# A graph-network layer on one core: the convolution's columns cut 128 + 6 x (133 or 134) instead of 116 + 6 x (135 or 136)

## The chip, the cores and the metric

The kernel runs on one core of a Trainium2 chip. The metric is the device time of one execution in microseconds, as the median of several runs. Engines are named as the profile names them: PE (TensorE matmuls), PEld (its weight loads), DVE (VectorE), ACT (ScalarE), POOL (GpSimd) and SP (SyncE, which issues most of the DMAs).

## What is computed

The input `x` has 32 batches of 512 nodes with 256 features, and `adj` is a 512 x 512 mask for each batch. All is in float32. Cut to what matters:

```python
h  = relu(layernorm(x))
# conv branch, along the nodes
c  = relu(bn1(conv1(h)))             # 1 tap, 256 -> 256
xc = relu(bn2(conv2(c)) + h)         # 17 taps, padding 8
# graph branch
s  = h @ w_se.T + b_se               # 3 numbers per node
A  = exp(-dist(s, s)) * adj
xn = A @ relu(h @ w_msg.T + b_msg)
# gates
gi = concat(xc, xn) @ w_ih.T + b_ih ; gh = h @ w_hh.T + b_hh
r, z = sigmoid(gi_r + gh_r), sigmoid(gi_z + gh_z)
out = x + (1 - z) * tanh(gi_n + r * gh_n) + z * h
```

## The kernel before

**The convolution by columns.** The 17-tap convolution is done with 25 products per group of columns in place of 17 (a bilinear scheme with five points, twice, on top of a split into two phases). A unit is 18 consecutive nodes (`Q = 18`), a batch has 29 units (`U = 29`), and the 32 batches give 928 columns in one row. `STARTS` cuts these 928 columns into seven groups, and cuts need not fall between batches; a batch on a cut has columns in two groups. `batches(g)` lists the batches that group `g` touches.

For each group, in this order:

- `rows(g, b)` calls `conv1(g, b, o)` for each batch and output half: PE multiplies `w1` by the batch's normalized, transposed rows (`hT`, [128 x 2 x 512]) into a `ps_g` bank, and ACT writes the result with batch norm and relu into `h1`, the one buffer that holds the group's input. In group 0 the rows are still in SBUF; in the others `load_row` loads them again from the DRAM copy `hd` (512 KB, on SP's queue). The tile `hT` has two buffers, also used when a batch is first transposed.
- `operands(g)` makes the 25 operands (`x2`, and for groups above 0 also their difference `xd`) on DVE from `h1`. It can begin when all rows of the group are there (`made`), and the next group's rows can be written when the last outer operand of this one has been read (`freed`). At most three operands are made ahead (`AHEAD = 3`).
- `convolution()` runs the 25 products into `ps_c`. Group 0 takes two half products of 8 matmuls each per operand (4 each for the operand `LONE`), while the weights are still being made on DVE and ACT; the later groups take three products of 4 matmuls (two for `LONE`) with weights that SP loads back from DRAM (`w<-wd`). Each matmul has as many columns as the group.
- `summed(g)` adds the products up on ACT and DVE (`n`, `z`, `y`), and `evacuate()` writes them as `part` and, on POOL's queue, to DRAM as `cd`.

**The other work.** `begin(b)` normalizes batch `b` and turns it into `hT` and `hd`: by PE transposes for the first eight batches (`TURNED = 8`; the tiles `x_sb`, `x_odd` and, for batches 2 and 3, `y`), by DVE for the rest. `graph(b)` makes messages (`wmsg`), the kernel's exponentials (`right`, `left`), multiplies by the mask (`m_sb`, tile `at`) and gathers (`at,msg`). `gates(b)` does the gates (`ps_acc`), in a form with fewer products (`wsum`, `t`) for all batches but the first and last. It begins when the weights of group 0 are made.

**What sets the order.** The program is written out once, by a planner inside the kernel. It keeps an estimated time (`now`) and five streams: rows, begins, graphs, conv and gates. At each step it takes the stream that is furthest behind its due rate among those that could run. Wherever several could run, it counts one (`choices`), and the table `OTHERS` names the counts at which the second or third is taken instead. All engines, and the queues of SP and POOL, then work through that order. When no stream can run, `now` moves on in steps of 0.25 us; before the first gates, every fourth such step issues a 128 x 128 transpose of the identity, which does nothing but keep PE busy (`keep_warm`, line 272, `ps_acc<-ident`).

The streams' use of group 0 is in two places, `all_rows` and `all_begins`: the first `G = 4` batches are begun by the rows stream itself, each followed at once by its rows; all others by the begins stream.

Of the kernel before, what the change touches and what calls it, by code (L numbers as in the profile page):

```python
# [31 lines left out]
G = 4  # L32
U = 29
Q = 18

STARTS = (0, 116, 252, 388, 523, 658, 793, 928)
NG = len(STARTS) - 1
UG = max(j - i for i, j in zip(STARTS, STARTS[1:]))
PER = (STARTS[-1] - STARTS[1]) / (NG - 1) / U
TURNED = 8  # L40
# [10 lines left out]
def kernel(  # L51
# [32 lines left out]
    B, N, D = x.shape  # L84
# [4 lines left out]
    def sizes(g):  # L89


        nu = STARTS[g + 1] - STARTS[g]
        return nu, ND * nu, 2 * ND * nu, ND * (nu + 1)
# [190 lines left out]
    def later(t, f):  # L284
        LATER.append((t, f))
        LATER.sort(key=lambda e: e[0])
# [48 lines left out]
    def load_row(b):  # L335
        if b not in HR:
            settle_stores()
            HR[b] = front.tile([P, ND, N], F32, name="hT", bufs=2)
            sp.dma_start(HR[b], HD[b])
            HR_AT[b] = done(HR[b])  # L340
# [87 lines left out]
    def input_of(g):  # L428
        return h1[:, : Q * sizes(g)[3]].rearrange("p (q i v) -> p q i v", q=Q, i=ND)

    def zeros(g):
        at = input_of(g)
        for b in range(B + 1):
            v = U * b - STARTS[g]
            if 0 <= v <= sizes(g)[0]:
                pool.memset(at[:, : Q if v == sizes(g)[0] else LEAD, :, v : v + 1], 0.0)
                if v > 0:
                    pool.memset(at[:, Q - 1 : Q, :, v - 1 : v], 0.0)
# [91 lines left out]
    def conv1(g, b, o):  # L530

        hT = HT[b] if g == 0 else HR[b]
        v0, at = U * b - STARTS[g], input_of(g)
        first, last = max(0, -v0), min(U, sizes(g)[0] - v0)
# [363 lines left out]
    def batches(g):  # L898

        return range(STARTS[g] // U, (STARTS[g + 1] - 1) // U + 1)  # L900
# [332 lines left out]
    def begin(b):  # L1233

        nonlocal begun, turning
        if b >= TURNED:
            yield lambda: b not in NORMS
            yield NORM_AT[b]  # L1240
            xs = XS.pop(b)
            pool.dma_start(XD_[b].rearrange("(c p) d -> p c d", p=P), xs)
            yield done(XD_[b])
            xb = xs.rearrange("p c d -> p (c d)").rearrange("p (o n) -> p o n", o=ND)
            for o in range(ND):
                blocks(xb[:, o, :], XD_[b].rearrange("(k i) d -> i k d", i=32), o)
            yield max(done(xb), front.free("hT", 2))
            settle_stores()
            HT[b] = front.tile([P, ND, N], F32, name="hT", bufs=2)
            turning = True  # L1250
            for o in range(ND):
                dve.transpose(HT[b][:, o, :], xb[:, o, :])
                if o < ND - 1:
                    yield dve.free
            yield dve.free + 0.4
            pool.dma_start(HD[b], HT[b])
            begun, turning = b + 1, False
            if b + 1 < B:
                later(now + 0.3, lambda: load(b + 1))
            return  # L1260
        if b == 2:
            yield lambda: told > 0
        yield lambda: b not in NORMS
        yield NORM_AT[b]
        turning = True
        for d in range(ND):
            yield gps.free("ps_g")
            norm_t(b, d)
            if d == ND - 1:
                begun, turning = b + 1, False  # L1270
                if b < 2 or G <= b < TURNED - 1:
                    load(b + (G if b < 2 else 2))
            yield now

    def rows(g, b):
        nonlocal made, made_at
        for o in range(ND):
            yield gps.free("ps_g")
            conv1(g, b, o)
            if o == ND - 1 and b == batches(g)[-1]:  # L1280
                made, made_at = g + 1, act.free + LAG
            yield now
        HT.pop(b, None)
# [457 lines left out]
            yield from graph(b)  # L1741

    def all_begins():
        for b in range(G, B):
            yield lambda: b in XS and not rows_wait
            yield from begin(b)

# [1 line left out]

    def all_rows():  # L1750
        nonlocal rows_wait
        for b in range(G):
            yield from begin(b)
            yield act.free + LAG
            yield from rows(0, b)
        for g in range(1, NG):
            for b in batches(g):
                yield lambda: (
                    freed >= g - 1 and begun > b and not turning and at_product >= 25 * g - 4
                )  # L1760
                if b == batches(g)[0]:
                    zeros(g)
                rows_wait = True
                yield front.free("hT", 2) - 0.5
                load_row(b)
                if b + 1 in batches(g) and b + 1 < begun:
                    later(max(now + 2.5, front.free("hT", 2) - 0.5), lambda b=b: load_row(b + 1))
                yield HR_AT[b]
                yield from rows(g, b)
                del HR[b]  # L1770
                rows_wait = b + 1 in HR

    def all_gates():
# [6 lines left out]

    streams = {
        "rows": (all_rows(), 1e9, -2.0),
        "begins": (all_begins(), 1.05 * PER, -0.15),
        "graphs": (all_graphs(), 11.5 * PER, -0.5),
        "conv": (convolution(), 80.0, 0.0),
# [5 lines left out]


    OTHERS = {
        6: 1, 41: 1, 259: 1, 374: 1, 430: 1, 443: 1, 547: 1, 953: 1, 979: 1, 1020: 2,
        1022: 1, 1182: 1, 1202: 1, 1260: 1, 1291: 1, 1471: 1, 1636: 1, 1670: 1, 1744: 1,
        1745: 1, 1837: 1, 2031: 1, 2149: 1, 2232: 1, 2391: 1, 2604: 1, 2610: 1,
    }
    choices = 0
    unused, waits = acc.tile([P, N], F32, name="ps_acc"), 0
# [113 lines left out]
```

## Time and profile before

| | |
|---|---|
| median of 3 runs | 2008.96 us (2005.38 to 2012.02) |
| the profiled execution | 2015.27 us, of which its span is 2013.5 us |
| PE busy, DVE busy, ACT busy, POOL busy | 1973.8, 1505.0, 874.1, 478.5 us |
| mean granted clock of PE | 0.991 of full speed |
| group 0's products | from 55.5 us to 232.8 us |
| windows 0:60, 60:234, 234:1815, 1815:2013.5: PE busy | 52.94, 167.75, 1564.16, 188.97 us |
| the same windows: DVE busy | 38.93, 140.07, 1234.71, 91.27 us |

A row of the groups reads: line, engine, operation, output <- input, the tile sizes, the count; then busy time and mean length of one record in ns; then the idle time of the engine just before these, and what ended it. A row of the timeline reads: start, length of the stretch, engine, line, operation, count, and in brackets the idle time before it with what ended it. All matmuls come from the helper line 259 and PE transposes from 265, so groups are told apart by their tiles. A float32 matmul of the code is two records in the trace, each with its own weight load; the start of one to the start of the next is what it costs.

### The profile page before, as it was taken

Reading aid. Unit: us, or ns where it says so; the run is one execution under the profiler, and the core shown is the slowest. Engines: PE = TensorE matmul, PEld = TensorE weight load, DVE = VectorE, ACT = ScalarE, POOL = GpSimd, SP = SyncE. Lnnn points to the kernel's source line nnn. Section 1 sums busy time; section 2 is a strip of 40 time slices with the busy share of each in tenths; the row PEclk is TensorE's granted clock in tenths of the full one; section 3 lists DMA queues with packets and bytes.
Section 4 is the critical chain, followed back from the end, with each engine's and each line's share of the span. In section 5 each row is a group of like instructions: output and inputs, shape, how many; then the busy total and the mean of one; then the engine's idle time right before and its main releaser. Section 6 shows DMA issues by size and latency. Waiting matters only on the chain.

```text
span 2013.5 us, 28526 instructions
## 1 busy us (share of the span) xinstructions
PE 1973.8 (98%) x9692; PEld 1450.8 (72%) x9692; DVE 1505.0 (75%) x2711; ACT 874.1 (43%) x1755; POOL 478.5 (24%) x628
## 2 busy tenths in 40 slices
PE   8999999999999999999999999999999999999998
PEld 5887666776778677776787776777776777776774
DVE  6889589976988597876787775688894877766443
ACT  6644463434634455333464235463334453324321
POOL 3222112222212132222231221232220221113232
PEclk9999899999999999999999999999999999999999
DMA  8446777888898788889787886798895876665564
GB/s 295 168 174 211 238 241 194 211 209 197 227 252 208 194 191 213 200 195 222 146 235 192 204 202 162 191 246 203 179 211 150 185 171 155 157 151 106 111 100 34
DMA packets 578177, 378.92 MB, mean 188 GB/s; under 512 B 457664, under 2 KB 475488, under 8 KB 576896
## 3 DMA queue, kind: packets, MB, share of 16 engines
q1 hardware_dynamic: 419760, 279.15, 49.7%
q0 software_dynamic: 157184, 97.81, 26.4%
q8 instruction: 77, 1.26, 0.2%
q14 instruction: 68, 0.56, 0.1%
q10 hardware_dynamic: 1088, 0.13, 0.0%
HBM read 278.94 MB, written 114.56 MB: 195 GB/s over the span
## 4 chain that ended last, share of the span: by engine, by line
PE 65%; DVE 4%; issue 2%; DMA 1%; ACT 1%; POOL 1%; DVEq 0%; POOLq 0%; SPq 0%; ACTq 0%
PE ps_acc L259 36%; PE ps_c L259 16%; PE ps_g L259 13%; DVE o_sb L241 1%; DMA cd<-part 1%; PE ps_g L265 1%; DVE t L241 0%; POOL out_dram L228 0%; DVE x L241 0%; DMA hd<-hT 0%; POOL cd L228 0%; DVE ps_acc L241 0%; ACT at L241 0%; DVE z L241 0%; DMA w<-wd 0%
## 5 line engine op out<-in xcount | busy, mean ns | idle before, releaser
L228 POOL DMA_DIRECT2D out_dram<-o_sb x252 | 275.8, 1719 | 636.5 <-DVE o_sb L241 510.9
L259 PEld LDWEIGHTS ps_c<-xd,w 128*128 128x128 f32 x2304 | 285.5, 190 | 49.9 <-ACT ps_c L241 33.9
L259 PEld LDWEIGHTS ps_c<-x,w 128*128 128x128 f32 x2032 | 259.8, 194 | 48.2 <-issue 32.9
L259 PE MATMUL ps_c<-xd,w 128*128 128x135 f32 (+1 forms) x2304 | 290.4, 279 | 3.9 <-ACT ps_c L241 3.9
L259 PE MATMUL ps_c<-x,w 128*128 128x135 f32 (+2 forms) x2032 | 268.5, 281 | 2.8 <-DVE x L241 2.8
L259 PE MATMUL ps_g<-at,msg 128*128 128x512 f32 x512 | 230.0, 600 | 3.5 <-DVE at L241 3.5
L241 DVE TENSOR_TENSOR ps_acc<-ps_acc,r 128x256 f32<-128x256 f32 x120 | 51.7, 431 | 230.4 <-PE ps_acc L259 209.3
L259 PE MATMUL ps_acc<-hTb,whh 128*128 128x512 f32 (+2 forms) x532 | 211.4, 495 | 1.4 <-ACT r L241 1.4
L259 PE MATMUL ps_acc<-xconv,wih 128*128 128x512 f32 (+2 forms) x532 | 211.6, 495 | 0.7 <-DVE ps_acc L241 0.7
L259 PE MATMUL ps_acc<-xnb,wih 128*128 128x512 f32 (+2 forms) x532 | 209.1, 496 | 3.2 <-DVE ps_acc L241 3.2
L259 PEld LDWEIGHTS ps_g<-at,msg 128*128 128x128 f32 x512 | 96.9, 193 | 112.8 <-issue 103.4
L259 PE MATMUL ps_acc<-t,wsum 128*128 128x256 f32 x720 | 175.7, 380 | 1.2 <-DVE wsum L241 1.2
L259 PEld LDWEIGHTS ps_acc<-t,wsum 128*128 128x128 f32 x720 | 135.7, 191 | 35.5 <-issue 17.9
L259 PEld LDWEIGHTS ps_acc<-xconv,wih 128*128 128x128 f32 x532 | 98.0, 190 | 48.3 <-issue 38.6
L259 PE MATMUL ps_g<-hT,w 128*128 128x512 f32 (+8 forms) x296 | 124.5, 571 | 7.4 <-DMA hT<-hd 6.8
L259 PEld LDWEIGHTS ps_acc<-xnb,wih 128*128 128x128 f32 x532 | 96.1, 190 | 44.8 <-issue 31.5
L259 PE MATMUL ps_g<-wmsg,hTg 128*128 128x259 f32 x496 | 124.4, 382 | 0.0
L259 PE MATMUL ps_acc<-t,wih 128*128 128x256 f32 x480 | 123.2, 380 | 0.0
L259 PEld LDWEIGHTS ps_acc<-hTb,whh 128*128 128x128 f32 x532 | 94.7, 190 | 38.5 <-issue 28.3
L241 DVE TENSOR_TENSOR x<-x 128x544 f32<-128x544 f32 (+2 forms) x175 | 120.2, 707 | 0.3
L241 ACT ACTIVATE ps_c<-ps_c 128x270 f32<-128x270 f32 (+1 forms) x144 | 56.3, 391 | 137.9 <-PE ps_c L259 137.7
L241 ACT ACTIVATE h<-ps_g,bn_shift,bn_scale 128x252 f32<-128x252 f32 (+8 forms) x212 | 86.3, 484 | 60.4 <-PE ps_g L259 60.4
(157 smaller groups left out, 3251.3 us busy)
## 6 DMA issues: line engine op xcount, KB each, us to landing
w<-wd SPq DMA_DIRECT2D x414, 256.0 KB, 4.0
m_sb<-in_adj_dram SPq DMA_DIRECT2D x384, 64.0 KB, 3.4
wd<-w POOLq DMA_DIRECT2D x74, 256.0 KB, 3.3
hT<-hd SPq DMA_DIRECT2D x33, 512.0 KB, 4.0
hd<-hT POOLq DMA_DIRECT2D x32, 512.0 KB, 6.1
hTb<-hd SPq DMA_DIRECT2D x32, 512.0 KB, 4.6
xnb<-nd SPq DMA_DIRECT2D x64, 256.0 KB, 3.3
out_dram<-o_sb POOLq DMA_DIRECT2D x252, 64.0 KB, 4.8
```

Of the source, the lines that this page charges most:

```text
L228: self.engine.dma_start(dst, src, **more)
L241: getattr(self.engine, op)(*tiles, **more)
L259: nc.tensor.matmul(ps, lhsT, rhs, **more)
L265: nc.tensor.transpose(ps, a, ident)
```

## The change

The first cut moves from 116 (four whole batches) to 128, which is 12 columns into batch 4. The other six groups have 134, 134, 133, 133, 133 and 133 columns where they had 136, 136, 135, 135, 135 and 135. The first group thus touches five batches, and the two places that assumed `G = 4` batches ask `batches(0)` instead, so that batch 4 is begun by the rows stream. `OTHERS` is another table: 51 entries for 27.

```diff
-STARTS = (0, 116, 252, 388, 523, 658, 793, 928)
+STARTS = (0, 128, 262, 396, 529, 662, 795, 928)
...
     def all_begins():
-        for b in range(G, B):
+        for b in range(batches(0)[-1] + 1, B):
             yield lambda: b in XS and not rows_wait
             yield from begin(b)
...
     def all_rows():
         nonlocal rows_wait
-        for b in range(G):
+        for b in batches(0):
             yield from begin(b)
             yield act.free + LAG
             yield from rows(0, b)
...
     OTHERS = {
-        6: 1, 41: 1, 259: 1, 374: 1, 430: 1, 443: 1, 547: 1, 953: 1, 979: 1, 1020: 2,
...
+        85: 1, 89: 2, 121: 1, 157: 2, 194: 1, 260: 1, 280: 1, 344: 1, 347: 1, 404: 1,
...
     }
```

## The prediction, made before the changed kernel was run

> **What bounds the kernel.** I read the page first, then the windows, the groups by form, PE's waits and PE's timeline. TensorE is busy nearly throughout; nothing else is close.
>
> ```profile
> span 2013.5 us, 28526 instructions
> PE 1973.8 (98%) x9692; PEld 1450.8 (72%) x9692; DVE 1505.0 (75%) x2711; ACT 874.1 (43%) x1755; POOL 478.5 (24%) x628
> PE ps_acc L259 36%; PE ps_c L259 16%; PE ps_g L259 13%; DVE o_sb L241 1%; DMA cd<-part 1%; PE ps_g L265 1%; DVE t L241 0%; POOL out_dram L228 0%; DVE x L241 0%; DMA hd<-hT 0%; POOL cd L228 0%; DVE ps_acc L241 0%; ACT at L241 0%; DVE z L241 0%; DMA w<-wd 0%
> ```
>
> The chain of waits is PE work with few interruptions. So a column taken from PE counts in full, and other engines count only where PE waits for them. In the groups by form the convolution's products (ps_c) are:
>
> ```profile
> L259 PE MATMUL ps_c<-xd,w 128*128 128x135 f32 x1536 | 193.0, 279 | 3.2 <-ACT ps_c L241 3.1
> L259 PE MATMUL ps_c<-x,w 128*128 128x135 f32 x832 | 114.4, 282 | 0.0
> L259 PE MATMUL ps_c<-xd,w 128*128 128x136 f32 x768 | 97.4, 279 | 0.8 <-ACT ps_c L241 0.8
> L259 PE MATMUL ps_c<-x,w 128*128 128x116 f32 x784 | 96.8, 281 | 2.8 <-DVE x L241 2.8
> L259 PE MATMUL ps_c<-x,w 128*128 128x136 f32 x416 | 57.3, 281 | 0.0
> ```
>
> The mean of 280 ns is the length of overlapping records and says nothing of their price; the distance of starts does. (The code's 392 matmuls of 116 columns are 784 records: two for each matmul.)
>
> ```profile
> 91.17 1.94 PE L259 MATMUL ps_c<-x,w 128*128 128x116 f32 x16
> 92.95 0.60 PE L265 MATMUL ps_g<-ident,m_sb 128*128 128x128 f32 x4
> ...
> 553.53 2.02 PE L259 MATMUL ps_c<-xd,w 128*128 128x136 f32 x16
> 555.39 1.04 PE L259 MATMUL ps_g<-wmsg,hTg 128*128 128x259 f32 x4
> ```
>
> Sixteen records of 116 columns take 92.95 - 91.17 = 1.78 us, **111.3 ns** each; of 136 columns 1.86 us, **116.3 ns**. Over the trace the median is 115.0 for 135 columns and 429.4 for 512: a slope of 314.4/377 = 0.834 ns per column and 2.4 fixed. By it 116 columns would take 99.1; they take 111.3. Something else sets 12 ns of it, and up to about 130 columns come free.
>
> [...]
>
> ```profile
> 201.76 5.37 PE L259 MATMUL ps_g<-hT,w 128*128 128x512 f32 x8 [2.94 <-DMA hT<-hd]
> 206.96 0.27 PE L265 MATMUL ps_g<-ident,augl 128*128 128x128 f32 x1
> ...
> 237.15 10.20 PE L259 MATMUL ps_g<-at,msg 128*128 128x512 f32 x16 [2.36 <-DVE at L241]
> 247.19 1.04 PE L259 MATMUL ps_g<-wmsg,hTg 128*128 128x259 f32 x4
> ...
> 455.69 10.14 PE L259 MATMUL ps_g<-hT,w 128*128 128x512 f32 x16 [2.33 <-DMA hT<-hd]
> ```
>
> Eight records took 5.20 instead of 8 x 0.429 = 3.43; sixteen took 10.04 and 9.98 (to 465.67) instead of 6.87. So such a wait costs itself and 1.8 to 3.2 us more. These are the places where the convolution passes from one group to the next: the hT row loads (load_row) and the last adjacency mask.
>
> **The change, part by part.** The order of the changed kernel's instructions gives counts.
>
> 1. *Groups 1 to 6.* All of 1536 + 832 + 768 + 416 = 3552 records lose two columns: 3552 x 2 x 0.834 ns = **-5.9 us**, all on PE. At 133 columns the line gives 113.3, still above 111.3, so none of it is cut off. Bounds: if the floor reached 113.3, nothing changes; at 115, all of it is lost.
>
> 2. *Group 0.* 784 records grow from 116 to 128. The line gives 109.2, under the 111.3 paid now: **0**. Not shown in this stream, so bounded: -2.1 ns each (-1.6 us) if the line holds alone, +1.2 (+0.9 us) by the 112.5 of the few 128-column gate matmuls at the end.
>
> 3. *Rows.* Group ends move; batch 4 is now cut, so there is one piece more: 152 instead of 148 conv1 matmuls, 72 more columns (0.1 us) and an 89-column piece that pays the floor (0.3): **+0.4 us**. Row loads stay 33 (before: 37 pieces less 4 from SBUF; now 38 less 5). Two more evacuations on ACT and two more stores on POOL's queue lie beside PE: 43% and 24% busy.
>
> 4. *DVE.* From 638 ns at 468 elements to 717 at 544: 1.04 ns an element. [...] Group 0's operands and sums grow by 6,288 elements: +6.5 us; the others shrink by 7,872: -8.2. PE sees the first only if DVE is late there. DVE is idle 6.8 us in 60:100 and 6.6 in 100:150, which covers it; in 150:200 it is 96% busy and the two DVE waits of 0.56 and 1.75 us stand there. I take +1 (0 to +4).
>
> 5. *The start.* Operands wait for the whole group, which now includes batch 4. Its eight transposes (8 x 0.109) and four conv1 matmuls of 225 columns (8 x 0.19 = 1.5 us) move ahead of the first product (at 55.53 before), and the 0.5 us ACT evacuation and about 2.4 us of DVE operands follow. The order now puts graph 1's masks and gather (6.9 us) ahead of the first product too, where six short products filled PE between 55.5 and 71. Until the gather the new order has only some 5 us of work for about 10 us of latency. It holds eight more warm-up transposes (38 for 30), six of them at the start: 8 x 0.109 = **+0.9 us**, and a sign that its planner finds nothing for PE there. I take **+3** of idleness (1 to 6); the first products' cold clock (3.50 us for 1.78) may come back after it or vanish under the gather.
>
> 6. *Group changes.* Passing 0 to 1 costs now 2.94 + 1.77 (row load), 2.36 + 3.17 (mask), 1.15 of slow clock at 218.74 and 0.6 of short waits: 12.0 us. Passing 1 to 2 costs 0.58 + 2.33 + 3.11 = 6.0. In the new order 7.0 us of PE work, not 2.6, stand ahead of the second row batch of group 1, and four xd products part the last two masks. I take back the first row wait and some of the mask: -7 at 0 to 1. Passing 1 to 2, a load must now land within 4.3 us (below): half recovered, half lost elsewhere, 0. **-7 us** (-12 to +16).
>
> Sum: -5.9 + 0 + 0.4 + 1 + 3 + 0.9 - 7 = **-7.6 us** against the profiled execution's 2015.27 us (span 2013.5 and 1.8 around it): 2007.7. That execution stands 6.3 us over the median of the runs, 2008.96, so the forecast is 2008.96 - 7.6 = **2001.4 us**.
>
> **Rivals.** *The start eats it.* Part 5 at +6, part 6 at -4 because DVE, fed with group 1's long operations, is late for the mask again: -5.9 + 0.4 + 1 + 6 + 0.9 - 4 = -1.6, so 2007.4. For it: the six warm-ups, and the 1.35 us wait that precedes the first product already. Against it: batch 4's work is only moved.
>
> *Slower: exposed row loads.* hT has two buffers, so a row batch's load waits until the batch two before it is done. In the new order seven loads of groups 2 to 5 have only one batch (3.4 us) and about 0.9 us between release and use: 4.3 us. Before, such a load was just in time:
>
> ```profile
> 951.55 3.75 SPq L228 DMA_DIRECT2D hT<-hd  x2
> ...
> 954.79 1.02 PE L259 MATMUL ps_acc<-xconv,wih 128*128 128x512 f32 x2
> 955.68 6.15 PE L259 MATMUL ps_g<-hT,w 128*128 128x512 f32 x16
> ```
>
> Issued at 951.55, used at 955.68: 4.1 us and no wait. The median landing is 4.0, but transfers of hT range from 2.9 to 11.6. Each that is 2.3 us late costs 2.33 + 3.11 = 5.4. With two of the seven late the sum is about +3; with three it is -7.6 + 16.3 = +8.7: **2017.7**, and slower is decided there. Behind such a load SP holds weight loads, and behind PE's rows wait ACT's evacuation and DVE's next operands. Against it: the case above did not wait.
>
> *The cut does not pay.* If the floor holds 133 columns at 115 ns, part 1 is nothing and the sum is -1.7: 2007.3, like the first rival.
>
> **How the numbers follow.** About 0.3% (6.0 us, from 2002.9 to 2015.0) is what a measurement of this kernel tells from no change. The likeliest case is faster, 0.48: its own range is 1994 to 2003, with part 6 near its good end at 1996. The start or the floor eats the gain: 0.31. Exposed loads: 0.21. Leaving a tenth out on either side gives 1995 to 2018.
>
> **What would show it.** ps_c starts 113 to 114 ns apart at 133 and 134 columns and 109 to 112 at 128; a total of PE waits before the first product up by about 3 us; that first product near 72 us, not 55; the 2.94 us wait for hT gone; waits <-DMA hT<-hd otherwise under 7 us in all. I am wrong if 128 columns take over 113 ns, if those waits pass 15 us, or if DVE waits in group 0 exceed 6 us.

## The result, and the profile after

The changed kernel takes **2012.91 us** (median of 20 runs, 2009.14 to 2018.51); beside it on the same chip the kernel before takes 2008.17 us (20 runs, 2003.01 to 2014.92). The ratio is **1.0026**, 95% interval 1.0015 to 1.0036: slower by about 5 us. The prediction was 2001.4 us, and its sign was wrong.

The page after, its head and its chain of waits:

```profile
span 2010.9 us, 28562 instructions
PE 1966.8 (98%) x9708; PEld 1442.8 (72%) x9708; DVE 1500.9 (75%) x2711; ACT 875.9 (44%) x1761; POOL 477.0 (24%) x629
PE ps_acc L259 37%; PE ps_c L259 15%; PE ps_g L259 13%; DMA cd<-part 1%; DMA hT<-hd 1%; DVE o_sb L241 1%; DVE t L241 1%; PE ps_g L265 0%; ACT at L241 0%; ACT y L241 0%; DMA x_sb<-in_x_dram 0%; SPq L228 0%; DVE ps_acc L241 0%; ACT z L241 0%; POOL out_dram L228 0%
```

PE is still the bound at 98%, and busy for 7.0 us less than before. The trap is in the first line: this profiled span is 2.6 us shorter than the span shown of before. The profiled execution of before (2015.27 us) was slower than all 20 of its runs, the one of the change (2012.66) lies at its median. Two single profiles don't rank kernels that are 5 us apart; the runs do.

The convolution's products in the groups by form of the changed kernel (busy, mean ns of a record | idle time just before them and what ended it):

```profile
L259 PE MATMUL ps_c<-xd,w 128*128 128x133 f32 x1536 | 191.6, 277 | 3.8 <-ACT ps_c L241 3.8
L259 PE MATMUL ps_c<-x,w 128*128 128x133 f32 x832 | 112.1, 277 | 0.0
L259 PE MATMUL ps_c<-xd,w 128*128 128x134 f32 x768 | 96.5, 278 | 1.0 <-ACT ps_c L241 0.9
L259 PE MATMUL ps_c<-x,w 128*128 128x128 f32 x784 | 94.6, 276 | 1.2 <-ACT w L241 0.9 <-DVE x L241 0.3
L259 PE MATMUL ps_c<-x,w 128*128 128x134 f32 x416 | 57.0, 281 | 3.0 <-ACT z L241 1.6 <-DVE w L241 1.3
```

The last two rows show what is new. Group 0's products (128 columns) wait for DVE 0.3 us instead of 2.8, but group 1's `x` products, which never waited, now wait 3.0 us for ACT and DVE. The prices stand in PE's timeline after, as distances of starts:

```profile
199.13 3.73 PE L259 MATMUL ps_c<-x,w 128*128 128x128 f32 x32
202.70 2.22 PE L259 MATMUL ps_g<-hT,w 128*128 128x305 f32 x8
...
529.05 2.00 PE L259 MATMUL ps_c<-xd,w 128*128 128x134 f32 x16
530.89 0.59 PE L259 MATMUL ps_acc<-t,whh 128*128 128x256 f32 x2
...
1293.59 1.07 PE L259 MATMUL ps_c<-x,w 128*128 128x133 f32 x8
1294.50 1.04 PE L259 MATMUL ps_g<-wmsg,hTg 128*128 128x259 f32 x4
```

They are 3.57/32 = 111.6 ns for 128 columns, 1.84/16 = 115.0 for 134 and 0.91/8 = 113.8 for 133. Over all neighbouring product records of the trace at full clock the means are 111.7, 114.6 and 114.0, within 0.7 ns of the prediction's floor and line. Before, they are 111.3 for 116 columns, 116.5 for 136 and 115.0 for 135. In groups 1 to 6 that is 2368 x 0.96 + 1184 x 1.95 ns = 4.6 us of PE's time, for 5.9 predicted: over a quarter of the 133-column records take 117 or 118 ns, the rest 112 to 114.

**The start** is another matter. The windows of before, then of the change (the columns are the length, then busy time and records of PE, PEld, DVE, ACT and POOL, then granted clock, DMA share and GB/s):

```profile
0.00:57.00 57.00, 49.94 (x188) 30.43 (x189) 36.18 (x116) 38.13 (x83) 17.02 (x41) 0.96 0.75 275
57.00:80.00 23.00, 23.00 (x145) 18.92 (x145) 20.81 (x40) 9.78 (x24) 4.91 (x8) 0.96 0.43 149
80.00:250.00 170.00, 161.39 (x1007) 126.05 (x1006) 134.49 (x246) 86.10 (x201) 36.94 (x71) 0.96 0.63 208
```

```profile
0.00:57.00 57.00, 49.17 (x184) 29.20 (x184) 32.60 (x111) 38.12 (x84) 16.95 (x41) 0.96 0.74 275
57.00:80.00 23.00, 18.60 (x60) 11.81 (x61) 14.87 (x29) 6.31 (x14) 2.71 (x4) 0.73 0.41 149
80.00:250.00 170.00, 163.83 (x1114) 134.94 (x1113) 145.93 (x257) 91.81 (x216) 38.06 (x73) 1.00 0.57 188
```

Between 57 and 80 us PE was busy throughout before, with 145 records. After it is busy 18.60 us at a clock of 0.73, with 60. Up to 80 us PE thus has 5.2 us more of idleness, and the lower clock costs about (0.96 - 0.73) x 23 = 5 us. From 80 to 250 us the change does better: 163.83 us busy at full clock against 161.39 at 0.96, which is 2.4 us less idleness and about 7 us less of slow clock. So a loss at the start is followed by a gain, most of it at the passage from group 0 to group 1. PE's timeline shows the loss (brackets: idle time before the stretch, and what ended it). First before, then after:

```profile
55.53 3.67 PE L259 MATMUL ps_c<-x,w 128*128 128x116 f32 x16 [0.49 <-DVE x L241]
...
67.42 3.73 PE L259 MATMUL ps_c<-x,w 128*128 128x116 f32 x32
70.99 7.04 PE L259 MATMUL ps_g<-at,msg 128*128 128x512 f32 x16
```

```profile
54.18 0.69 PE L259 MATMUL ps_acc<-right,left 5*128 5x512 f32 x1 [1.25 <-ACT right L241]
...
57.10 1.97 PE L265 MATMUL ps_g<-ident,x_sb 128*128 128x128 f32 x8 [1.40 <-ACT at L241]
...
65.36 0.27 PE L272 MATMUL ps_acc<-ident 128*128 128x128 f32 x1
69.92 10.14 PE L259 MATMUL ps_g<-at,msg 128*128 128x512 f32 x16 [4.29 <-DVE at L241]
79.90 1.28 PE L259 MATMUL ps_c<-x,w 128*128 128x128 f32 x10
```

Graph 1's gather waits 4.29 us for its last mask, and then runs at a granted clock of 0.69 (0.50 up to 76.03 us): 9.98 us to the next start for 6.87. The first product stands at 79.90, not near 72. DVE's timeline in that stretch says why the mask is late:

```profile
65.49 0.39 DVE L241 BATCH_NORM_STATS2 st<-x_sb 128x6 f32<-128x256 f32 x1
...
66.74 0.68 DVE L241 TENSOR_TENSOR at<-ps_g,at 128x512 f32<-128x512 f32 x1
67.34 1.83 DVE L241 TENSOR_TENSOR x<-h 128x1290 f32<-128x1290 f32 x2
69.09 0.69 DVE L241 TENSOR_TENSOR at<-ps_g,at 128x512 f32<-128x512 f32 x1
```

Between the second and the last of the four mask multiplications (`at<-ps_g,at`) stand the next batch's statistics (64.42 to 66.74) and the first two operand instructions of group 0 (`x<-h`, 1.83 us together). Before, the gather came no earlier (70.99), but six products filled PE until then; now the products wait behind the gather, and PE has nothing to do until DVE is through.

And the gain, PE's timeline after at the passage from group 0 to 1:

```profile
202.70 2.22 PE L259 MATMUL ps_g<-hT,w 128*128 128x305 f32 x8
...
211.84 7.03 PE L259 MATMUL ps_g<-hT,w 128*128 128x512 f32 x16
218.70 1.95 PE L259 MATMUL ps_c<-x,w 128*128 128x128 f32 x16
...
247.64 7.13 PE L259 MATMUL ps_g<-at,msg 128*128 128x512 f32 x16 [1.11 <-DVE at L241]
...
256.05 1.15 PE L259 MATMUL ps_c<-x,w 128*128 128x134 f32 x8 [1.27 <-DVE w L241]
```

No row load is waited for, and the mask wait is 1.11 us with a gather at a granted clock of 1.00, where it was 2.36 with one at 0.69: as predicted. But 8 us later a new wait stands, for a weight that DVE makes (and DVE in turn waited 1.99 us for the load `w<-wd`).

**A ledger.** To add this up, I take PE's time up to a point and subtract the price, at full clock, of every record that PE has done by then: the mean distance of starts of its shape, and 0.53 us for four of the exponentials' records, which start within 0.02 us of one another (in the change from 54.18 us, the next four from 54.72). What is left is idleness and slow clock. The second value is that of a second profile (below).

| lost, us | up to 80 us | 80 to 250 us | 250 us to the end |
|---|---|---|---|
| before | 18.0, 18.5 | 18.5, 16.7 | 45.0, 44.2 |
| the change | 28.1, 29.0 | 9.9, 9.9 | 43.9, 52.9 |
| held116 | 19.5 | 18.6 | 38.7 |
| masks128 | 24.3 | 10.8 | 44.3 |
| masks128_stats | 20.6 | 11.4 | 44.2 |
| order128 | 27.5 | 11.5 | 37.7 |
| order128_held | 25.6 | 9.9 | 37.1 |
| order128_stats | 22.1 | 11.5 | 38.2 |

So the change loses about 10 us more than before by 80 us, gets 7 to 9 back by 250, and is then 1 to 4 us behind. The last column varies by 9 us between two executions of one kernel, and both profiles of before are of executions 5 to 7 us over the median of its runs. An estimate at the medians of the runs: PE's work is 1932.0 us before and 1929.1 after, so 74.4 and 82.0 us are lost in all (with 1.8 us around the span), and some 38 and 44 of them behind 250 us. There the change loses about 5 us more.

### The profile page after: what moved, and what is told of

Same layout as the page of the kernel before. It is cut to its first block, busy times and chain, and to the rows that moved or that the text cites. A ratio compares the mean times of both kernels' runs of the same rounds, so it can differ in the third digit from the quotient of the medians.

```text
span 2010.9 us, 28562 instructions
## 1 busy us (share of the span) xinstructions
PE 1966.8 (98%) x9708; PEld 1442.8 (72%) x9708; DVE 1500.9 (75%) x2711; ACT 875.9 (44%) x1761; POOL 477.0 (24%) x629
## 4 chain that ended last, share of the span: by engine, by line
PE 66%; DVE 3%; DMA 2%; issue 2%; ACT 2%; POOL 1%; SPq 0%; DVEq 0%; POOLq 0%; ACTq 0%
PE ps_acc L259 37%; PE ps_c L259 15%; PE ps_g L259 13%; DMA cd<-part 1%; DMA hT<-hd 1%; DVE o_sb L241 1%; DVE t L241 1%; PE ps_g L265 0%; ACT at L241 0%; ACT y L241 0%; DMA x_sb<-in_x_dram 0%; SPq L228 0%; DVE ps_acc L241 0%; ACT z L241 0%; POOL out_dram L228 0%
## 5 line engine op out<-in xcount | busy, mean ns | idle before, releaser
L259 PEld LDWEIGHTS ps_c<-x,w 128*128 128x128 f32 x2032 | 254.3, 190 | 58.2 <-issue 40.2
L259 PE MATMUL ps_c<-xd,w 128*128 128x133 f32 (+1 forms) x2304 | 288.1, 277 | 4.8 <-ACT ps_c L241 4.8
L259 PE MATMUL ps_c<-x,w 128*128 128x133 f32 (+2 forms) x2032 | 263.6, 278 | 4.2 <-ACT z L241 1.6
L259 PEld LDWEIGHTS ps_acc<-xconv,wih 128*128 128x128 f32 x532 | 96.6, 190 | 44.2 <-issue 35.9
L259 PE MATMUL ps_g<-hT,w 128*128 128x512 f32 (+10 forms) x304 | 118.8, 539 | 2.8 <-DMA hT<-hd 2.5
L241 DVE TENSOR_TENSOR x<-x 128x536 f32<-128x536 f32 (+2 forms) x175 | 120.2, 707 | 0.3
L241 ACT ACTIVATE ps_c<-ps_c 128x266 f32<-128x266 f32 (+1 forms) x144 | 55.8, 388 | 129.3 <-PE ps_c L259 128.9
L241 ACT ACTIVATE h<-ps_g,bn_shift,bn_scale 128x252 f32<-128x252 f32 (+12 forms) x216 | 88.0, 481 | 52.2 <-PE ps_g L259 52.0
```

Source lines behind the costliest of these rows:

```text
L241: getattr(self.engine, op)(*tiles, **more)
L259: nc.tensor.matmul(ps, lhsT, rhs, **more)
```

## The experiments

My theory after the result: the columns pay as predicted, and the order eats more than that, at the start and later on. Rival A: the shorter records don't pay. Rival B: the passages between groups were only unlucky in the profile of before, so there was nothing to regain. Rival C: row loads are exposed.

**Second profiles of both.** No edit.

> The kernel before once more, for its waits: the profile shown of it was taken of an execution 6 us over the median. Theory of the unlucky profile: the waits of 2.94, 2.36 and 2.33 us at the group changes and the half clock after them (18 us in all with the short ones) are not all there in another execution; 6 us or more of them are gone. Otherwise they recur within 2 us.

> The changed kernel once more. Theory of the start: the wait of about 4.3 us for the mask before graph 1's gather and the half clock after it recur, and by 80 us PE has lost 9 to 11 us more than in the kernel before. Theory of the order: the start's loss varies, and the difference lies in waits of 0.5 to 2 us from 100 us on.

Measured: 2013.15 us (span 2011.4) and 2022.5 us (span 2020.7). The waits of before recur: 2.00 us for hT at 203.57, 2.36 for the mask at 237.29, 1.25 for hT at 436.70, and 1.53 ahead of the rows at 454.45, which ACT ends this time and no row load. So does the change's 4.29 us wait (at 70.89). But most of what the slow clock behind the waits of before cost (granted there: 0.67, 0.69 and 0.69) doesn't recur: the rows at 203.57 take 3.51 us for 5.20, the gather at 237.29 8.65 for 10.04, the rows at 454.45 6.94 for 9.98. By the prediction's way of counting the two passages cost about 10 us there and not 18, so 6 us or more are gone, as the first theory of the expectation had it. Rival B is half right: there was something to regain, but less than the one profile shows.

(The expectations here and below price the ledger more coarsely: in them the change has lost 24.7 us by 80 us and 41 behind 250.) The page after also settles rival C; in this row, all row products of the change, only 2.5 us of idleness are ended by a row load:

```profile
L259 PE MATMUL ps_g<-hT,w 128*128 128x512 f32 (+10 forms) x304 | 118.8, 539 | 2.8 <-DMA hT<-hd 2.5
```

**narrow116: the columns alone.** The order of before; the products of groups 1 to 6 lose the last two columns of each half (these stay uncomputed), and one 272-column matmul is added.

```diff
+                cut = 2 if wide else 0
...
-                        ps[:, o * nu : (o + 1) * nu], lhsT, rhs,
+                        ps[:, o * nu : (o + 1) * nu - cut], lhsT, rhs[:, : nu - cut],
```

> The kernel before with its order of all instructions kept (one extra 272-column matmul at the start of group 1), but every product of groups 1 to 6 leaves out its last two columns of each half: 134 and 133 columns instead of 136 and 135. The columns alone. If a column saved on PE counts in full: 3552 records x 1.67 ns = 5.9 us faster than before (ratio 0.997), and product starts 113.3 to 115 ns apart. If the saving is absorbed by waits that grow elsewhere: less than 3 us.

Measured: 2002.75 us against 2008.6, ratio 0.9977 [0.9968, 0.9987]: **-4.6 us**. Rival A is out. But this run is kinder to the columns than the change: its products start 113.3 and 114.2 ns apart, on the prediction's line, where the changed kernel with the same widths has 114.0 and 114.6. PE's product time falls by 6.7 us here (0.6 go to the added matmul), in groups 1 to 6 of the change by 4.6. Why the changed kernel's records are longer is open.

**held116: the start alone.** Cut and columns of before, the order written out as a fixed list of streams; the first 11 steps of conv (products of six operands) are moved behind graph 1's gather, as in the change.

```diff
-        "...g14r6gr5gcgcb3g2b2cg2b2c3g2cg2b3c4g11b2c3gc..."
+        "...g14r6gr5g2b3g2b2g2b2g4b3g4c11g7b2c3gc..."
```

> The kernel before (cut 116, its own order), with one thing moved: the first six of group 0's operands' products, which stood between the exponentials and the gather of graph 1, are held until that gather is issued. The start alone, without batch 4's rows. Theory of the start (PE has lost its filler there, waits over 4 us and runs at half clock after it): 6 to 10 us slower than before, with a long wait before the gather near 68 us and the gather at half clock. Theory of the order (the loss is spread over the whole new order): within 2 us of before.

Measured: 2013.26 us against 2008.6, ratio 1.0021 [1.0012, 1.0031]: **+4.3 us**. In its timeline the gather comes early and hardly waits:

```profile
62.36 7.13 PE L259 MATMUL ps_g<-at,msg 128*128 128x512 f32 x16 [0.43 <-DVE at L241]
69.33 10.87 PE L259 MATMUL ps_c<-x,w 128*128 128x116 f32 x96
```

The ledger has it only 1 to 2 us behind before at 80 us, and 2 to 3 at 250. So the expected long wait isn't there, and the time lies between the two theories: giving up the products as filler costs PE even where no long wait appears.

**held_narrow116: both.** The two edits above in one kernel, with the same columns left out.

> The order of the kernel before, with both single parts of the change at once: group 0's operands and products held until graph 1 is gathered, and the products of groups 1 to 6 two columns narrower (their last two columns of each half are left out, and one 272-column matmul is added). Alone the columns gave -4.6 us and the held start +4.3. If what the cut brings and costs by itself adds up and the rest of the change's loss belongs to the new order, this is 0 +/- 2 us against before, ratio 0.999 to 1.001. If the two parts work on each other (a PE that is faster in groups 1 to 6 runs into waits that the late start has set up), it is as slow as the change, 1.002 to 1.0035. If held products are made up for later, as the trace of the held kernel suggests by itself (span below before's), it is 0.997 to 0.999.

Measured: 2005.01 us against 2006.99, ratio **0.9999** [0.999, 1.0008]. The two parts add up within the intervals (-4.6 + 4.3 = -0.3 expected, -0.2 measured; by the medians, of which the ratio here isn't the quotient, -5.9 + 4.7 = -1.2 and -2.0). The change does these two things, and costs 1.0026; some 5 us of it are something else. By the ledger's prices 2.5 of these 5 are PE work, 1929.1 us in the change for 1926.6 here, most of it columns that pay less.

**masks128: the change, with long operands behind the masks.** On DVE alone, the two long operand instructions (1.83 us together) come after graph 1's last masks.

```diff
+        if not masks_made:
+            return False
```

(in `operand_some`; `masks_made` is set when graph 1's last mask is issued.)

> The changed kernel with the order of every engine and queue kept, except on DVE at the start: the first two operand instructions of group 0 (2 x 1.83 us) and one of 0.69 us come after the last two mask multiplications of graph 1 instead of before them. Theory of the start: the 4.29 us wait before graph 1's gather shrinks to about 1 us and its half clock (3.1 us) goes, so 5 to 7 us faster than the changed kernel, about 1.000 of the kernel before. Theory of the order: within 2 us of the changed kernel, 1.002 to 1.003 of the kernel before.

Measured: 2012.14 us against 2007.8, 1.0019 [1.0011, 1.0027]. (Where an expectation here or below counts 2 x 1.83 us, I had misread the timeline: 1.83 is the length of the stretch of two.) The wait ahead of the gather fell from 4.29 to 2.54 us and the gather took 7.11 us, as at full clock (7.13 at 247.64 in the change, granted 1.00), as expected; but 5 to 7 us were expected of it, the ledger shows 3.8 by 80 us, and the runs some 1.4, within the noise.

**masks128_stats: the next batch's statistics behind the masks as well.**

```diff
     def norm_ahead():
+        if masking and not masks_made:
+            return False
```

> The changed kernel with graph 1's four mask multiplications ahead of everything else on DVE: as in masks128, and the next batch's statistics (4 x 0.5 us and two small ones) put behind them too. PE's wait ahead of the gather, 4.29 us in the change and 2.54 in masks128, should fall to about 0.5 us. If a microsecond at the start is a microsecond at the end, it is 2 us below masks128 (1.0019): 1.001 or less. If the start's loss is mostly given back later, it stays at 1.0015 to 1.002, and the order behind the start makes the difference of 5 us between held_narrow116 and the change.

Measured: 2009.74 us against 2007.54, 1.0011 [1.0004, 1.0019]. PE's timeline:

```profile
63.89 0.49 PE L272 MATMUL ps_acc<-ident 128*128 128x128 f32 x3
64.98 7.10 PE L259 MATMUL ps_g<-at,msg 128*128 128x512 f32 x16 [0.60 <-DVE at L241]
71.92 3.73 PE L259 MATMUL ps_c<-x,w 128*128 128x128 f32 x32
```

The first product now stands at 71.92. With PE's order unchanged but for the warm-ups, the start loses 7.5 us less by 80 us (some 2 of them are slow clock ahead of the gather, granted 0.68 from 57.10 to 65.36 in the change, that this profile happens not to have: its 225-column rows take 1.69 us for 2.57) and the kernel gains (1.0026 - 1.0011) x 2008 = 3 us. The intervals of the two ratios overlap a little, but the steps go one way (1.0026, 1.0019, 1.0011). So about 3 of the missing 5 us, with 2 to 3 us of doubt, are the DVE order at the start, and what is won there is in part lost again later.

**Other orders.** `OTHERS` is exchanged for another table.

- order116, cut 116: `227: 2, 482: 2, 750: 2, 1996: 1`
- order128, cut 128: `258: 1, 534: 1, 589: 1, 1047: 1, 1313: 1, 1848: 1, 1940: 1, 2272: 1, 2545: 1`
- masks_order128, cut 128, operands behind the masks as in masks128: `259: 1, 523: 2, 641: 2, 1083: 1, 1161: 1, 1893: 1`
- p116, cut 116: the table of before and `704: 1, 776: 1, 1014: 2, 1337: 1`

> The cut of the kernel before (116) with another table made anew from none (4 entries). If orders are worth several microseconds by themselves, it differs from the kernel before by 3 us or more either way although not one column is moved; if the cut alone decides, within 2 us. By 80 us PE has lost 13 to 14 us either way.

> The cut of the changed kernel (128) with another table of exchanged places, made anew from none (9 entries); the same start, other orders from about 80 us on. Theory of the start (the cut costs it, whatever the order): by 80 us PE has lost 24 to 25 us as in the changed kernel, and the time is 1.001 to 1.005 of the kernel before. Theory of the order (the changed kernel's table is merely an unlucky one): the time can fall to 0.998, with the loss after 250 us at 36 us or less instead of 41.

> Cut 128, masks of graph 1 ahead of the first operands on DVE, and a table made anew for it (6 entries). Theory of the start and of the order together: 0.996 to 1.000 of the kernel before, since the columns' 5 us remain. Theory that the cut costs more than the start: 1.001 or more.

> The cut and table of the kernel before, with four more entries in the table at choices 704, 776, 1014 and 1337. The start is before's to the instruction. If single entries in the middle of the program are worth single waits, this is within 3 us of before, 0.9985 to 1.0015; if any change in the order sets all later waits anew, as the tables made from nothing did, it can be 3 to 20 us slower, 1.0015 to 1.01.

Measured: order116 2032.91 us, 1.0119 [1.01, 1.0137]; order128 2010.38, 1.0011 [1.0002, 1.0021]; masks_order128 2018.51, 1.0053 [1.0039, 1.0067]; p116 2010.07, 1.0023 [1.001, 1.0036]. With the cut held, the order moves the time from -3 us (order128 against the change, with intervals that overlap) to +24 (order116 against before); four added entries make +4.6. The hope for masks_order128, 0.996 to 1.000, failed: with masks128's start and another table it is 7 us slower than masks128. The page of order116 has the prediction's slower rival in it: row loads that are waited for 17.9 us.

```profile
L259 PE MATMUL ps_g<-hT,w 128*128 128x512 f32 (+8 forms) x296 | 122.0, 559 | 18.0 <-DMA hT<-hd 17.9
```

**A better order at the same cut.** order128 has the same 4.29 us wait at 69.74 us. The two DVE edits are applied to it: order128_held has the edit of masks128, order128_stats both.

> The cut at 128 with the other table of 9 entries (1.0011 measured), and in it the two long operands (2 x 1.83 us on DVE) put behind graph 1's last two masks; nothing else changes its place. PE's 4.29 us wait ahead of graph 1's gather should shrink to about 2.5 and the gather take 7.1 instead of 9.8 us: 4 to 5 us by 80 us. If the start is paid for in full at the end, -4 us against the other table alone: 0.999. If the later waits take most of it back, as they did with the change's own table (1.4 us came through of 4.6), -1 us: 1.000 to 1.001.

> The same step on order128_held (cut 128, the other table, long operands behind the masks; 0.9991 measured): the statistics behind the masks as well. Full pass-through: -2 us, 0.998. Given back later: 0.9985 to 0.9995.

Measured: order128_held 2004.81 us against 2006.99, 0.9991 [0.998, 1.0001]; order128_stats 2004.54 against 2007.54, **0.9986** [0.9975, 0.9997]. From 1.0011 to 0.9986 is 5 us, by DVE's order in the first 70 us. order128_stats beats both kernels, by about 3 us of before and 8 of the change. Its start has the same steps as that of masks128_stats (the gather with a wait of 0.60 us, then the first products), and by the ledger loses no less by 80 us (22.1 for 20.6); between the two lie 5 us of order behind it. The ledger's last column agrees: 37 to 38 us in three profiles with this table, 44, 44, 44 and 53 in four with the change's.

## Why the prediction was wrong, point by point

**Columns (part 1): the mechanism right, the size four fifths.** -5.9 us predicted, 4.6 us less PE time by the distances of starts in the change; narrow116 measured -4.6 with a larger saving in PE time (6.1 net). **Group 0 (part 2): right**, 111.7 ns for 128 columns against 111.3 for 116, which is 0.3 us. The rival that the cut doesn't pay is out with both. **Rows (part 3): right**, 0.4 us more PE work by the ledger's prices.

**DVE in group 0 (part 4): covered as predicted, but for the place not looked at.** After 80 us PE waits for DVE 1.1 us in group 0 and 2.4 just behind it, where it was 5.1 in the same stretch before. With the 4.29 us ahead of the gather, group 0 has 5.4, close to the 6 that the prediction set as its limit. That wait belongs to the next part.

**The start (part 5): the first step that failed.** "I take +3 of idleness (1 to 6)", with 0.9 of warm-ups. By the ledger the start loses 10 us, about 5 as idleness (4.29 in one wait) and about 5 by the slow clock (3.1 right behind that wait); the warm-ups' 0.9 come on top. The prediction's own figures, some 5 us of work for about 10 us of latency, gave the idleness; it took 3. It counted DVE's operands as latency that the order leaves uncovered, but didn't ask what stands ahead of graph 1's last mask on DVE: 2.3 us of statistics and 1.8 us of operands. Nor did it put a term for the half clock, which it had priced elsewhere at 1.8 to 3.2 us a wait; it named it for the first products alone. At the end of the kernel the start costs +4.3 (held116) and about +3 (masks128_stats), if the two add up: 7 us for 3.9.

**Group changes (part 6): the second step that failed.** The gain at 0 to 1 came: the row wait is gone, and from 80 to 250 us the ledger gets 7 to 9 us back, for 7 taken. (That it fits is in part luck: the 18 us were read from a slow execution.) What failed is to count that gain as the part's whole result. "Half recovered, half lost elsewhere, 0" stood for passing 1 to 2 and nothing for what follows, and that is a new order of 1750 us of work, in which the change loses about 5 us more than before. So the part nets -2 to -4 by the ledger, and not -7.

Put together: PE's work falls by 3 us (columns -4.6, group 0 +0.3, rows +0.4, warm-ups +0.9); lost are 10 more by 80 us, 7 to 9 less by 250 and about 5 more behind it. The sum is the measured +5, since the last term is what the medians leave over. The experiments, which count what a step is worth at the end, say much the same of the order: masks128_stats has the change's order with a mended start, and held_narrow116 the columns and a late start in the order of before. By 80 us they have lost about the same (20.6 and 20.1 us). They differ by 1.0011 - 0.9999, +2.4 us, give or take 2.4, and 2.6 us of PE work are in that (1929.2 for 1926.6). So the order behind the start, with its gain at 0 to 1 in it, comes to about nothing in the end, and not to -7. The part's range, -12 to +16, was nearer the truth than the value taken from it.

Waits that the trace of before doesn't have at these places are in the change's timeline:

```profile
526.74 1.18 PE L259 MATMUL ps_c<-x,w 128*128 128x134 f32 x8 [1.57 <-ACT z L241]
...
596.40 0.69 PE L259 MATMUL ps_c<-right,left 5*128 5x512 f32 x1 [1.90 <-ACT n L241]
...
597.47 1.42 PE L259 MATMUL ps_c<-x,w 128*128 128x134 f32 x8
```

Eight records take 1.21 us there for 0.92, at a granted clock of 0.83. Both waits recur in the change's second profile (1.54 and 3.04 us) and in masks128_stats (1.65 and 2.52). That they make up the 5 us behind 250 us is argued, not shown; the scatter of single profiles is larger than that. Shown is that the order alone is worth it: masks128_stats and order128_stats have one cut and one start, and differ by 0.0025, 5 us.

**The rivals.** "The start eats it" had the right mechanism with the wrong size: +6 for the idleness, and 2007.4 for the time. "Exposed row loads" ended on the right side by the wrong mechanism: 2.5 us of such waits in the change. (Its range of 2.9 to 11.6 us for transfers of hT takes in the stores `hd<-hT`; in the trace of before the row loads alone take 3.1 to 7.3.) No rival said that another order by itself can cost as much as the cut brings; that was the case to be priced on the slower side.

## What to carry to other kernels

When a change replaces a hand-tuned or searched order, its effect is that of the new order in all of the program, and the old profile's waits tell little of it: give that a range of its own, from how much other orders of the same work move the time. When filler is taken from the bounding engine, look up, on every other engine, what stands ahead of the instruction that it waits for next; here 2.3 us of statistics and 1.8 us of operands on DVE made a 4.29 us wait. Compare kernels that differ by a few us with runs, and use a profile only for what recurs in a second one: of the 18 us that the prediction read at two passages, almost 8 did not.

## What the runs showed of the hardware

The slow clock doesn't follow from the length of the wait. A wait of 2.36 us (before, at 237) and one of 4.29 us (the change) were followed by gathers at a granted clock of 0.69, about 10 us for 6.87. In the second profile of before the same wait was followed by 8.65 us:

```profile
237.29 8.81 PE L259 MATMUL ps_g<-at,msg 128*128 128x512 f32 x16 [2.36 <-DVE at L241]
245.94 1.04 PE L259 MATMUL ps_g<-wmsg,hTg 128*128 128x259 f32 x4
```

Behind a wait of 2.54 us the change's gather took 7.11 us in masks128 and 8.80 in order128_held:

```profile
61.10 2.87 PE L259 MATMUL ps_g<-hT,w 128*128 128x225 f32 x8
...
68.81 8.80 PE L259 MATMUL ps_g<-at,msg 128*128 128x512 f32 x16 [2.54 <-DVE at L241]
77.44 3.73 PE L259 MATMUL ps_c<-x,w 128*128 128x128 f32 x32
```

There the work ahead of the wait was slow already: 2.87 us for rows that take 1.69 in masks128_stats. In the trace of the change the granted clock is 0.50 in five stretches, from 28.25, 55.55, 69.21, 598.27 and 1311.66 us, and in one that ends the trace. Each of the five lasts 3.413 or 6.827 us, and the later ones start 8, 12, 167 and 376 times 3.413 us after the first. In the trace of before there are eight such, of the same two lengths, and the later ones start 8, 51, 56, 61, 125, 349 and 470 times 3.413 us after the first. What sets these times is not shown. Waits of 2.3 to 2.6 us cost between 2.6 us (masks128) and 5.5 us (before, at 237) here; that it matters where between such stretches a wait falls is my estimate, which no run tests. The prediction priced this half clock for the group changes and left it out at the start.
